# Gated slot attention with a Hadamard feed-forward on one core: VectorE's work around the quarter-array products in another order

## The chip, the cores and the metric

The kernel runs on one core of one Trainium2 chip. The metric is device time of one execution in microseconds (us). Before the change the median of three runs was 3658.88 us (3658.03 to 3659.67). TensorE is called PE, VectorE DVE, ScalarE ACT, GpSimd POOL and SyncE SP, as in the profile; SP issues all DMAs. "Lnnn" is line nnn of the kernel before the change.

## The reference, cut to what matters

The input x is 2 x 2048 x 512 in float32. The block is an attention, a layer norm over the sum with x, a feed-forward, and a second layer norm over that sum:

```python
q, k, s = heads of x@Wq, x@Wk, clip(x@Ws, -32, 32)     # 16 heads of 64
v, g    = heads of x@Wv, x@Wg                          # 16 heads of 128
# gated slot attention: two linear recurrences over time, a softmax between them
z  = cumlogsumexp(s); p = exp(s - z); decay = exp(z[t-1] - z[t])
hk = hk*decay + k p^T ;  ok = q hk ;  pv = softmax(ok)
hv = hv*decay + p v^T ;  o  = pv hv
o = rmsnorm(o)*g_norm_weight * silu(g)
x = layernorm(x + o@Wo)
h = fwht(silu(x@W1.T) * (x@W3.T))                      # Walsh-Hadamard, 2048 wide
out = layernorm(x + h@W2.T)
```

## The kernel before

**Products.** All large products are done by Strassen's scheme in Winograd's form, with 7 block products in place of 8 and two levels of it in the feed-forward. Each product therefore needs sums of blocks of its left and right factors. `Weights.sums(k)` makes the four sums of a weight (L416 to L422), `right_factor` those of an activation (L443 to L449: two copies on ACT, two differences on DVE, two on POOL).

**Stages.** Attention comes first, in 64 steps: 4 groups of 4 heads, 16 chunks of 128 tokens (of both batches) in each group. The output rows are kept in DRAM (`yd`) and added to group by group, so only the fourth group's steps finish a row: there `row_stats` (L86 to L91: two DVE instructions for each batch, then two short POOL instructions) and `normalize` (L95) do the layer norm, and `rows_transposed` (L914) or `rows_transposed_last` (L930) turn the rows for the feed-forward. Preparation of the feed-forward's weights (`up_weights` in group 0, `down_weights` after it) and of its input blocks (`block`, in group 3) is cut into pieces that are run inside the attention steps. The feed-forward (`up`, `down`) follows.

**Order.** The order on PE, DVE, ACT and POOL is exactly the order in which the code calls things; SP's is arranged by the framework. Each engine works through its queue in order. `run(new, now, before, old)` writes one iteration, in which four steps overlap: it loads for `new`, projects and scores `now`, finishes `before` (second recurrence, gate, transposition, first output products) and ends `old` (last output products, rows out). `main("q", k)` and `main("v", k)` are the seven products of the two projections (L519, L545), and everything else stands between them. `next(pieces[0])` runs one piece of preparation; an iteration has four such places, here called place 2 (after q2), 3 (after q5), 4 (after q6) and the end. In the last four chunks `more()` adds four places among the v products.

**The places that the change touches**, in the order of an iteration:

- q products, output products `old.o` 3, 6 and 7 (`o`, L754 is the DVE addition that empties their PSUM bank).
- `exp_s` (L527 on DVE, L531 and L533 on ACT, L532 on POOL), then v1, `load_rows`, `k_transposed` (L565), `old.o(4)`, `e_transposed` (L571) and `running_sum` (L578), which reads what L532 has written.
- "Quarter-array products": matmuls of 64 x 64 blocks (`scores` L596, `scores2` L669, `share_of_keys` L604, `slots` L622, `share_of_values` L679, `values` L690, `state_slots` L631, `state_values` L699), and the first half of `reciprocal` (L589).
- `gated`: ACT squares (L716), DVE multiplies by the gate (L718), `state` (L616 into `hv`), DVE sums the squares (L721), POOL makes the factor (L722, L723) and multiplies the gated values by it (L725).
- v6, v5, second `reciprocal`, v2, `row_stats` of `old`, v7, `softmax` (L639 reads the PSUM tile `pn`, L645, L647 on DVE, L648 on ACT), `store_rows` of `old` with `normalize`, v3, `softmax_sum` (L652, L653 on DVE, L654 on POOL).
- `o_transposed` (L742): PE transposes the gated values into PSUM and `right_factor` makes `ob` of them (L443 and L444 on ACT, L446 and L447 on DVE, L448 and L449 on POOL).
- `softmax_end` (L658), v4, `tanh`, `before.o` 1, 5, `silu` (L559), 2 (L758 is the matmul of all `o`).

**PSUM.** Two double banks `ps[0]` and `ps[1]` serve everything but the products' sums. `flat(0)` is all of `ps[0]`, `flat(2)` all of `ps[1]`. `pn`, which `softmax` reads, lies in `ps[1]`; so did the transposed gated values, `flat(2)`. `state` reads the second half of `ps[0]`. The products' sums rotate over four banks: `c1` (two), `c2` and `c3`; o1 uses c1, o5 and o3 c2, o2 c3.

Of the kernel before, what the change touches and what calls it, by code (L numbers as in the profile page):

```python
# [9 lines left out]
F32 = mybir.dt.float32  # L10
# [28 lines left out]
def gated_slot_attention_ffn_kernel(  # L39
# [43 lines left out]
    def row_stats(src):  # L83

        st = small.tile([P, 6], F32, name="st")
        nc.vector.bn_stats(st, src)  # L86
# [263 lines left out]
    with ExitStack() as att:  # L350
# [16 lines left out]
        def flat(at):  # L367
            return ps[at // 2].rearrange("p b (i t) -> p (b i) t", t=P)
# [22 lines left out]
        class Weights:  # L391
# [17 lines left out]

            def sums(self, k):  # L410
                t, low = self.t, self.low
                if k == 0:
                    if self.raw is not None:
                        self.raw(t[:, 0:3])
                        self.raw(low)
                    nc.vector.tensor_tensor(t[:, 3], low, t[:, 2], ALU.add)  # L416
                elif k == 1:
                    nc.vector.tensor_tensor(t[:, 5], t[:, 0], low, ALU.subtract)
                elif k == 2:
                    nc.vector.tensor_tensor(t[:, 4], t[:, 3], t[:, 0], ALU.subtract)  # L420
                else:
                    nc.vector.tensor_tensor(t[:, 6], t[:, 1], t[:, 4], ALU.subtract)  # L422

        def rows_of(src, g, width):
            return lambda j: src[j * HD : (j + 1) * HD, g * width : (g + 1) * width]
# [53 lines left out]
        class Step:  # L479
# [228 lines left out]
            def gated(self):  # L708

                sq = c1.tile([P, 2, NQ, DV], F32, name="sq", tag="big")  # L710
                self.gj = self.t2[:, :, HD:].rearrange("p q (j d) -> p j q d", d=DV)

                every = slice(0, P)
                moves = [(0, every, every), (1, HALVES[0], HALVES[1]), (1, HALVES[1], HALVES[0])]
                for j, to, at in moves:
                    nc.scalar.activation(sq[to, j], self.po[j][at], AF.Square)  # L716
                for j, to, at in moves:
                    nc.vector.tensor_tensor(self.gj[to, j], self.po[j][at], self.gj[to, j], ALU.mult)  # L718
                self.state()
                ss = small.tile([P, 2 * NQ], F32, name="ss")  # L720
                nc.vector.tensor_reduce(ss, sq.rearrange("p j q d -> p (j q) d"), AX.X, ALU.add)  # L721
                nc.gpsimd.tensor_scalar(ss, ss, 1.0 / DV, EPS, ALU.mult, ALU.add)  # L722
                nc.gpsimd.tensor_tensor(ss, ss, mhalf, ALU.pow)  # L723
                ssb = ss.rearrange("p (j q o) -> p j q o", j=2, o=1).to_broadcast([P, 2, NQ, DV])
                nc.gpsimd.tensor_tensor(self.gj, self.gj, ssb, ALU.mult)  # L725


            def load_rows(self):
                self.rows = []
                for b in range(2):  # L730
                    t = yp.tile([P, D], F32, name="rows", tag="rows")
                    n = self.n
                    nc.sync.dma_start(out=t, in_=yd[b * NCB + n] if self.g else x[b, n * P : (n + 1) * P, :])
                    self.rows.append(t)

            def o_transposed(self):
                tp = flat(2)
                for b in range(2):
                    for i in range(2):
                        for j in range(2):  # L740
                            at = HD + j * DV
                            nc.tensor.transpose(  # L742
                                tp[:, b * 4 + i * 2 + j, :], self.t2[:, 2 * i + b, at : at + DV], ident
                            )
                self.ob = c1.tile([P, 7, 2, P], F32, name="ob")
                right_factor(self.ob, tp)
# [13 lines left out]
                        start=(k in OPENS and c == 0), stop=(c == 1), skip_group_check=True,  # L760
                    )

            def row_stats(self):
                if self.g == NG - 1:
                    self.stats = [row_stats(t) for t in self.rows]

            def store_rows(self):
                for b in range(2):
                    if self.g == NG - 1:
                        normalize(self.rows[b], self.stats[b])  # L770
                    nc.sync.dma_start(out=yd[b * NCB + self.n], in_=self.rows[b])


# [23 lines left out]
        def up_weights():  # L797

            todo = [(p, i, half) for p in range(NSET) for i in range(2) for half in range(2)]

            def load(p, i, half):
                return [load_row((w1, w3)[i], p + NSET * (2 * half + q)) for q in range(2)]

            def inner(d, src, at, n):

                t = hp.tile([P, 4, 2, P], F32, name="inner", tag="h3", bufs=4)[:, :, 0:n]
                first_sums(nc.vector, t, *(src(r, c) for r in range(2) for c in range(2)))
                o = d[:, at : at + n].rearrange("p m k t -> p k m t")
                for c in range(2):
                    nc.sync.dma_start(out=o[:, c], in_=src(0, c))  # L810
                nc.sync.dma_start(out=o[:, 2], in_=src(1, 1))
                for k in range(4):
                    nc.sync.dma_start(out=o[:, 3 + k], in_=t[:, k])

            def inners(d, wt, outer):
                inner(d, lambda r, c: wt[:, 0, r, :, c], 0, 2)
# [5 lines left out]
                inner(d, lambda r, c: outer[:, 2:4, r, c], 5, 2)  # L822

            raws, rest = load(*todo[0]), iter(())

            both = hp.tile([P, 2, 2, 2, 2, 2, P], F32, name="both", tag="h1")
            for n, (p, i, half) in enumerate(todo):
                next(rest, None)
                yield
                wt = both[:, n // 2 % 2]  # L830
                tp = ps[1].rearrange("p q (c t) -> p q c t", t=P)
                for q in range(2):
                    for c in range(KC):
                        nc.tensor.transpose(tp[:, q, c], raws[q][:, c * P : (c + 1) * P], ident)
                nc.scalar.copy(wt[:, half].rearrange("p i a b t -> p i (a b) t"), tp)
                next(rest, None)
                yield
                next(rest, None)
                if half:
                    outer = hp.tile([P, 4, 2, 2, P], F32, name="outer", tag="h2")  # L840
                    first_sums(nc.vector, outer, *(wt[:, r, :, c] for r in range(2) for c in range(2)))
                    rest = inners(w13s[p][:, :, :, i], wt, outer)
                yield
                if n + 1 < len(todo):
                    raws = load(*todo[n + 1])
                yield
            for _ in rest:
                yield

        def down_weights():  # L850
# [3 lines left out]
            for pair in ((0, 2), (1, 3)):  # L854
# [39 lines left out]
                for hb in range(NPB):  # L894
# [9 lines left out]
                    nc.sync.dma_start(out=o[:, 3:7], in_=t)  # L904
                    if hb % 2:
                        yield

        def rows_transposed(step):

# [87 lines left out]
                yield  # L997
            yield from down_weights()

        y = {"second": False}  # L1000
        pieces = [work()]
        ups = None
        steps = [Step(g, n) for g in range(NG) for n in range(NCB)]
# [2 lines left out]
        def run(new, now, before, old):  # L1006
# [6 lines left out]
            def main(name, k):  # L1013
# [3 lines left out]
                elif before is not None:  # L1017
                    for _ in range(FILL[name, k]):
                        next(ups)

            def more():

                if old is not None and old.g == NG - 1 and old.n >= NCB - 4:
                    next(pieces[0], None)


            g = now.g if now is not None else NG
# [17 lines left out]
            next(pieces[0], None)  # L1045
            if changes:
                nw["vg"].sums(0)
            main("q", 5)
            next(pieces[0], None)
            if changes:  # L1050
                nw["vg"].sums(1)
            main("q", 6)
# [2 lines left out]
            if changes:  # L1055
                nw["vg"].sums(2)
            main("q", 7)
            next(pieces[0], None)
# [56 lines left out]
            more()  # L1115
            if o_opens:
# [138 lines left out]
```

## Time and profile before

| What | Value |
|---|---|
| median of three runs | 3658.88 us |
| the profiled execution's own time | 3661.32 us |
| its span | 3659.5 us |
| PE busy, share of the span | 3512.5 us, 96% |
| DVE busy | 2380.8 us, 65% |
| POOL, ACT busy | 1088.0 us (30%), 987.4 us (27%) |
| mean granted TensorE clock | 0.996 |
| attention / feed-forward | up to about 2580 us / the rest |

The busy shares say that PE is nearly always at work. What PE is not at work is 147 us, and the view of waits names the releaser of most of it. A group's "idle before" is the time that its engine stood still just before it, and the releaser is the instruction whose end let it go. All but a few of PE's waits lie in the attention steps, of which one lasts about 40 us.

### The profile page before, as it was taken

The page shows a single profiled execution, that of the slowest core. Times are in us where ns is not written, and L with a number is a line of the kernel's source. Part 1 is how long each engine was busy: PE and PEld are TensorE (multiplying, and loading weights), DVE is VectorE, ACT ScalarE, POOL GpSimd, SP SyncE. Part 2 cuts the span into 40 slices and gives each one's busy share as a digit, 9 for nine tenths or more (in the row PEclk, how much of TensorE's full clock was granted, in tenths as well). Part 3 has the DMA queues.
Part 4 walks back from the last instruction along what each step waited for, and adds up shares of the span by engine and source line. Part 5 has one row for each costly group of instructions (what it writes and reads, how often), then busy time and mean ns, then how long its engine had stood idle before and what let it go on. Part 6 is the DMA issues. An engine that isn't in the chain of part 4 may idle for free.

```text
span 3659.5 us, 76139 instructions
## 1 busy us (share of the span) xinstructions
PE 3512.5 (96%) x32160; PEld 2774.9 (76%) x32160; DVE 2380.8 (65%) x3976; ACT 987.4 (27%) x1768; POOL 1088.0 (30%) x1040
## 2 busy tenths in 40 slices
PE   8999999999999999999999999998899999999998
PEld 6777776677777767777766776776688888888887
DVE  5667667755667655667566567767666765765756
ACT  3333333333333333333333333332111111111110
POOL 2222222211212221213112222222344454453553
PEclk9999999999999999999999999999999999999999
DMA  4433443411121321122121232435646535435432
GB/s 152 124 111 103 129 128 110 130 62 59 60 68 54 118 70 58 60 68 82 53 88 57 68 108 87 152 132 190 230 135 222 196 119 211 158 120 211 157 123 82
DMA packets 229190, 425.10 MB, mean 116 GB/s; under 512 B 20592, under 2 KB 141808, under 8 KB 228848
## 3 DMA queue, kind: packets, MB, share of 16 engines
q1 hardware_dynamic: 228848, 420.22, 34.5%
q8 instruction: 253, 4.15, 0.5%
q14 instruction: 89, 0.73, 0.1%
HBM read 297.47 MB, written 125.30 MB: 116 GB/s over the span
## 4 chain that ended last, share of the span: by engine, by line
PE 75%; DVE 12%; POOL 5%; ACT 3%; issue 3%; DMA 1%; SPq 0%; POOLq 0%; DVEq 0%; ACTq 0%
PE c L235 17%; PE c L519 16%; PE dc L274 10%; PE c L758 10%; PE c L545 6%; ACT sq L716 3%; DVE t L718 2%; POOL t L725 2%; POOL ss L723 2%; DVE ss L721 2%; PE ps L679 2%; PE po L699 2%; PE po L690 2%; PE running L578 2%; PE ps L742 1%
## 5 line engine op out<-in xcount | busy, mean ns | idle before, releaser
L545 PE MATMUL c<-wvg,xb 128*128 128x512 f32 x1792 | 814.5, 600 | 2.4 <-DVE wvg L420 1.8
L545 PEld LDWEIGHTS c<-wvg,xb 128*128 128x128 f32 x1792 | 324.5, 191 | 365.5 <-issue 293.9
L519 PE MATMUL c<-xb,wqks 128*128 128x128 f32 x3584 | 550.3, 276 | 5.6 <-DVE t L477 2.4
L519 PEld LDWEIGHTS c<-xb,wqks 128*128 128x128 f32 x3584 | 481.5, 192 | 23.6 <-issue 8.1
L274 PE MATMUL dc<-w2t,hid 128*128 128x256 f32 x1792 | 455.3, 379 | 2.1 <-DVE res L281 2.1
L216 DVE TENSOR_TENSOR accux<-c,accux 128x512 f32<-128x512 f32 x496 | 340.9, 690 | 177.9 <-PE c L235 161.9
L235 PE MATMUL c<-wvg,xb 128*128 128x256 f32 x1792 | 432.0, 380 | 7.3 <-DVE accux L216 6.5
L754 DVE TENSOR_TENSOR rows<-c,rows 128x256 f32<-128x256 f32 x448 | 182.1, 417 | 351.0 <-PE c L758 350.9
L235 PEld LDWEIGHTS c<-wvg,xb 128*128 128x128 f32 x1792 | 338.7, 190 | 58.3 <-DVE accux L216 10.3
L274 PEld LDWEIGHTS dc<-w2t,hid 128*128 128x128 f32 x1792 | 340.2, 190 | 49.5 <-DVE res L281 3.3
L519 PE MATMUL c<-wqks,xb 128*128 128x128 f32 x1792 | 347.6, 276 | 1.1 <-DMA wqks<-in_L_attn_Ws 1.1
L477 DVE TENSOR_TENSOR t<-c,kept 128x384 f32<-128x384 f32 (+1 forms) x384 | 230.6, 609 | 165.1 <-PE c L519 157.8
L235 PE MATMUL c<-wqks,xb 128*128 128x256 f32 x1344 | 324.9, 380 | 6.8 <-DVE accv L216 2.5
L472 ACT COPY kept<-c 128x384 f32<-128x384 f32 (+1 forms) x384 | 203.1, 529 | 360.2 <-PE c L519 275.4
L532 POOL TENSOR_TENSOR e<-e,zc 1x512 f32<-1x512 f32 x60 | 75.9, 1264 | 754.4 <-ACT e L531 710.8
L235 PEld LDWEIGHTS c<-wqks,xb 128*128 128x128 f32 x1344 | 253.9, 190 | 45.7 <-DVE accux L216 5.2
L722 POOL TENSOR_SCALAR ss<-ss 128x8 f32<-128x8 f32 x64 | 13.1, 204 | 899.8 <-DVE ss L721 899.8
L519 PEld LDWEIGHTS c<-wqks,xb 128*128 128x128 f32 x1792 | 273.0, 193 | 1.4 <-DMA wqks<-in_L_attn_Ws 1.4
L281 DVE TENSOR_TENSOR res<-dc,res 128x256 f32<-128x256 f32 x448 | 188.8, 422 | 118.1 <-PE dc L274 107.3
L589 DVE RECIPROCAL iz<-z 128x256 f32<-128x256 f32 x128 | 223.2, 1744 | 0.0
L718 DVE TENSOR_TENSOR t<-po,t 64x512 f32<-64x512 f32 (+1 forms) x192 | 132.3, 689 | 122.1 <-ACT sq L716 121.3
L250 POOL TENSOR_TENSOR accw<-accw,accux 128x512 f32<-128x512 f32 x60 | 75.8, 1275 | 283.5 <-DVE accux L216 282.1
(194 smaller groups left out, 5116.7 us busy)
## 6 DMA issues: line engine op xcount, KB each, us to landing
xb<-w13s SPq DMA_DIRECT2D x112, 896.0 KB
xb<-xd SPq DMA_DIRECT2D x48, 896.0 KB
yd<-rows SPq DMA_DIRECT2D x128, 256.0 KB
w2t<-w2s SPq DMA_DIRECT2D x32, 896.0 KB
rows<-yd SPq DMA_DIRECT2D x100, 256.0 KB
xd<-xb SPq DMA_DIRECT2D x16, 896.0 KB
wvg<-fxd SPq DMA_DIRECT2D x16, 896.0 KB
raw<-in_L_ffn_W SPq DMA_DIRECT2D x48, 256.0 KB
```

What stands on the lines that cost most here:

```text
L216: nc.vector.tensor_tensor(into[:, b], s, (into if first is None else first)[:, b], ALU.add)
L235: nc.tensor.matmul(s[:, j * TQ : (j + 1) * TQ], lhsT=w[:, LEFT[k], j, :], rhs=right[:, RIGHT[k], :], start=(k in (1, 2, 5) and j == 0), st ...
L274: nc.tensor.matmul(s, lhsT=h["hid"][:, i, LEFT[m], k * P : (k + 1) * P], rhs=h["w2"][:, i, RIGHT[m], :], start=(m in (1, 2, 5) and i == 0) ...
L281: nc.vector.tensor_tensor(r, s, r, ALU.add)
L472: nc.scalar.copy(self.kept[k], s)
L477: nc.vector.tensor_tensor(t[:, to], s, self.kept[other], ALU.add)
L519: nc.tensor.matmul(out[:, i * P : (i + 1) * P], lhsT=a, rhs=b, start=(k in OPENS and c == 0 and i == 0), stop=(c == 1), skip_group_check=True,
L545: nc.tensor.matmul(out, lhsT=self.xb[:, RIGHT[k], c, :], rhs=w["vg"].t[:, LEFT[k], c, :], start=(k in OPENS and c == 0), stop=(c == 1), sk ...
L589: nc.vector.reciprocal(self.iz[:, h], self.z[:, h])
L718: nc.vector.tensor_tensor(self.gj[to, j], self.po[j][at], self.gj[to, j], ALU.mult)
L754: nc.vector.tensor_tensor(y_, self.uo.sum(k), y_, ALU.add)
L758: nc.tensor.matmul(out, lhsT=self.ob[:, RIGHT[k], c, :], rhs=w["o"].t[:, LEFT[k], c, :], start=(k in OPENS and c == 0), stop=(c == 1), ski ...
```

## The change

Six things are different.

1. `gated`: the sum of squares (L721) goes ahead of `state` (L616).
2. `o_transposed`: the gated values are transposed into `flat(0)`, not `flat(2)`.
3. `row_stats` is called for one batch at a time: for batch 1 right after `old.o(7)`, ahead of `exp_s`, for batch 0 right after `old.o(4)`. `normalize` becomes a call of its own, and it and `store_rows` go from behind `softmax` to behind the first half of `reciprocal`. As before, statistics and normalization happen in group 3 alone; the store, in all groups.
4. `Weights.sums`: for Wo, and only for it, sums 1 and 3 are made on POOL.
5. `up_weights`: of a pair of halves, the first sums, which stood together at place 4 (four instructions), are split over the end of the iteration and place 2 of the next; the inner sums follow at place 3, the end, place 2 and place 3. Place 4 has none. The whole preparation ends one iteration later.
6. `down_weights`: the pieces of the last sums skip place 4.

```diff
@@ Weights.sums
+                second = nc.vector if self.raw is None else nc.gpsimd
...
-                    nc.vector.tensor_tensor(t[:, 5], t[:, 0], low, ALU.subtract)
+                    second.tensor_tensor(t[:, 5], t[:, 0], low, ALU.subtract)
...
-                    nc.vector.tensor_tensor(t[:, 6], t[:, 1], t[:, 4], ALU.subtract)
+                    second.tensor_tensor(t[:, 6], t[:, 1], t[:, 4], ALU.subtract)
@@ gated
-                self.state()
                 ss = small.tile([P, 2 * NQ], F32, name="ss")
                 nc.vector.tensor_reduce(ss, sq.rearrange("p j q d -> p (j q) d"), AX.X, ALU.add)
+                self.state()
@@ o_transposed
-                tp = flat(2)
+                tp = flat(0)
@@ row_stats, store_rows
-            def row_stats(self):
+            def row_stats(self, b):
                 if self.g == NG - 1:
-                    self.stats = [row_stats(t) for t in self.rows]
+                    self.stats[b] = row_stats(self.rows[b])
+
+            def normalize(self):
+                if self.g == NG - 1:
+                    for b in range(2):
+                        normalize(self.rows[b], self.stats[b])

             def store_rows(self):
                 for b in range(2):
-                    if self.g == NG - 1:
-                        normalize(self.rows[b], self.stats[b])
                     nc.sync.dma_start(out=yd[b * NCB + self.n], in_=self.rows[b])
@@ up_weights
-            def inners(d, wt, outer):
+            def sums(d, wt):
+
+                outer = hp.tile([P, 4, 2, 2, P], F32, name="outer", tag="h2")
+                a11, a12, a21, a22 = (wt[:, r, :, c] for r in range(2) for c in range(2))
+                nc.vector.tensor_tensor(outer[:, 0], a21, a22, ALU.add)
+                nc.vector.tensor_tensor(outer[:, 2], a11, a21, ALU.subtract)
+                yield
+                nc.vector.tensor_tensor(outer[:, 1], outer[:, 0], a11, ALU.subtract)
+                nc.vector.tensor_tensor(outer[:, 3], a12, outer[:, 1], ALU.subtract)
+                yield
+                inner(d, lambda r, c: wt[:, 1, r, 1:2, c], 2, 1)
+                yield
+                inner(d, lambda r, c: outer[:, 0:2, r, c], 3, 2)
+                yield
+                inner(d, lambda r, c: outer[:, 2:4, r, c], 5, 2)
+                yield
                 inner(d, lambda r, c: wt[:, 0, r, :, c], 0, 2)
...
                 next(rest, None)
                 yield
+
+                yield
+                if half:
+                    for _ in rest:
+                        pass
+                    rest = sums(w13s[p][:, :, :, i], wt)
                 next(rest, None)
-                if half:
-                    outer = hp.tile([P, 4, 2, 2, P], F32, name="outer", tag="h2")
-                    first_sums(nc.vector, outer, *(wt[:, r, :, c] for r in range(2) for c in range(2)))
-                    rest = inners(w13s[p][:, :, :, i], wt, outer)
-                yield
@@ down_weights
                     if hb % 2:
                         yield
+                        if y["place"] == 3:
+                            yield
@@ run
             do(old, "o", 7)
+            do(old, "row_stats", 1)
...
             do(old, "o", 4)
+            do(old, "row_stats", 0)
...
             do(now, "reciprocal", 0)
+            do(old, "normalize")
+            do(old, "store_rows")
             do(before, "values")
...
-            do(old, "row_stats")
...
             do(now, "softmax")
-            do(old, "store_rows")
```

More of the change, by code (lines that the diff above doesn't have):

```diff
@@ L728, in load_rows @@
             def load_rows(self):
-                self.rows = []
+                self.rows, self.stats = [], {}
                 for b in range(2):
@@ L813, in inner @@
                     nc.sync.dma_start(out=o[:, 3 + k], in_=t[:, k])
-            def inners(d, wt, outer):
-                inner(d, lambda r, c: wt[:, 0, r, :, c], 0, 2)
+            def sums(d, wt):
[6 more added lines that the diff above has]
+                nc.vector.tensor_tensor(outer[:, 3], a12, outer[:, 1], ALU.subtract)
                 yield
@@ L822, in inners @@
                 inner(d, lambda r, c: outer[:, 2:4, r, c], 5, 2)
+                yield
+                inner(d, lambda r, c: wt[:, 0, r, :, c], 0, 2)
             raws, rest = load(*todo[0]), iter(())
@@ L846, in up_weights @@
                 yield
-            for _ in rest:
+            for place in range(4):
+                if place != 2:
+                    next(rest, None)
+                yield
+            for place in range(4):
+                if place != 2:
+                    next(rest, None)
                 yield
@@ L998, in work @@
             yield from down_weights()
-        y = {"second": False}
+        y = {"second": False, "place": 0}
         pieces = [work()]
@@ L1019, in main, with work_on @@
                         next(ups)
+            def work_on(place):
+                y["place"] = place
+                next(pieces[0], None)
             def more():
                 if old is not None and old.g == NG - 1 and old.n >= NCB - 4:
-                    next(pieces[0], None)
+                    work_on(1)
             g = now.g if now is not None else NG
@@ L1044, in run @@
             y["second"] = new is not None and new.g > 0
-            next(pieces[0], None)
+            work_on(2)
             if changes:
@@ L1048, in run @@
             main("q", 5)
-            next(pieces[0], None)
+            work_on(3)
             if changes:
@@ L1057, in run @@
             main("q", 7)
-            next(pieces[0], None)
+            work_on(4)
             if changes:
```

## The prediction

> **What bounds the kernel now.** I read the page's busy shares first: PE works 96% of the span, so a change on other engines can only give back what PE stands still, and the view of PE's waits prices that. Columns: waiting line, releaser, total us, times, longest.
>
> ```profile
> PE ps L742 <- DVE r L639: 35.2, 17, 5.1
> PE ps L742 <- POOL t L725: 17.1, 42, 0.4
> PE c L758 <- DVE ob L446: 11.1, 15, 2.7
> PE ps L631 <- issue: 11.1, 10, 2.6
> ```
>
> Two of the three upper lines are waits of the transposition L742 that the change attacks: for softmax's reading of `ps[1]` and for the gated values. The timeline splits them into kinds. An ordinary step of groups 0 to 2:
>
> ```profile
> 1032.81 1.90 POOL L725 TENSOR_TENSOR t<-t,ss 128x1024 f32<-128x1024 f32 x1
> 1033.44 0.68 DVE L639 TENSOR_TENSOR r<-ps,iz 128x512 f32<-128x512 f32 x1
> ...
> 1034.76 1.09 PE L742 MATMUL ps<-ident,t 128*128 128x128 f32 x8 [0.38 <-POOL t L725]
> ```
>
> and one of group 3, with the statistics in DVE's queue ahead of softmax:
>
> ```profile
> 2202.81 0.68 DVE L86 BATCH_NORM_STATS2 st<-rows 128x6 f32<-128x512 f32 x1
> ...
> 2205.01 0.68 DVE L639 TENSOR_TENSOR r<-ps,iz 128x512 f32<-128x512 f32 x1
> ...
> 2205.83 1.06 PE L742 MATMUL ps<-ident,t 128*128 128x128 f32 x8 [1.50 <-DVE r L639]
> 2206.73 1.88 PE L545 MATMUL c<-wvg,xb 128*128 128x512 f32 x4
> 2207.05 1.00 DVE L95 TENSOR_SCALAR rows<-rows,mv,lrs 128x512 f32<-128x512 f32 x2
> 2207.22 0.63 ACT L648 ACTIVATE r<-r 128x512 f32<-128x512 f32 x1 [7.43 <-DVE r L647]
> 2207.76 0.57 ACT L443 COPY ob<-ps 128x512 f32<-128x512 f32 x1
> ```
>
> The last two lines matter most: the copy L443 that makes o1's factor stands behind softmax's exponential L648 in ACT's queue, and L648 waits for DVE's L647. So even if L742 waits for softmax no longer, o1, four matmuls later, still waits for DVE through ACT. A freed L742 is worth only what that chain leaves.
>
> **The change part by part.** All times are of the profiled execution (3661.3 us; 2.4 above the median 3658.9; the differences are carried over).
>
> *A. Squares ahead of `state`, ordinary steps.* `state` (L616, 0.69) no longer stands ahead of L721, so the factor and L725 end about 0.6 us sooner; `state` comes 1.1 later and only empties half of `ps[0]`, next written by L742 itself 3 us on. In the step shown, the values are there at 1034.1 and PE is free at 1034.38: the 0.38 goes. What is late next: v4 then ends at 1037.03; `ob` L443 ends at 1036.77 as before, and o1 starts 0.12 after such an end (2208.33 to 2208.45). L446 ends at 1037.55, o5 needs it at 1037.9. Both fit, by 0.1 and 0.3. So 41 waits go whole: 17.1 less the 0.34 of the last, **-16.8**. Bounds: if the DVE chain slips by 0.15 only 0.24 a step is left (-10); nothing here can gain more.
>
> *B. Statistics and normalization moved, group 3.* Twelve steps wait 1.50 to 1.87 for L639 (sum 18.6) and 0.32 each for L446 at o5 (3.8). With the two pairs of L86 and L88 gone from the queue (2202.81 to 2204.42, 1.61 us) L647 ends at 2205.5 and L443 at 2206.7, o1 could start at 2206.83 and PE is there at 2206.95; without L95 (0.91) ahead of it L446 ends at 2207.5, o5 needs it at 2207.8. So 22.4 go. They are paid in another place. Batch 1's pair (0.82, and 0.1 for waiting on the end of L754) now stands ahead of `exp_s` L527, and what waits behind it is L531, L532 and `running_sum` L578, and L533 and `e_transposed`:
>
> ```profile
> 2186.19 0.63 ACT L531 ACTIVATE e<-e 128x512 f32<-128x512 f32 x1 [1.24 <-DVE e L527]
> 2186.90 1.27 POOL L532 TENSOR_TENSOR e<-e,zc 1x512 f32<-1x512 f32 x1 [14.23 <-ACT e L531]
> ...
> 2188.59 1.03 PE L578 MATMUL running<-e,causal 128*128 128x256 f32 x4
> ```
>
> L532 ends at 2188.17 and L578 starts at 2188.59: 0.37 of slack with 0.05 for the signal. L527 comes 0.94 later, so L578 waits 0.57; L571 takes 0.33 of that earlier. On POOL the pair L90, L91 (0.19 and 0.54) now stands ahead of L532, but ends at 2187.6, before the late L531 (2187.8): nothing. Batch 0's pair falls between o4 (L754 at 2188.36) and L598 (1.63 idle before it); both L95 fall into the 0.95 that DVE waits for L716: covered, the second by almost nothing. The stores go to SP some 10 us sooner with their rows. 12 x 0.57 = 6.8, so 18.6 + 3.8 - 6.8 = **-15.6**. Bounds of the price: 0 to 1.5 a step (all of 0.94, and POOL's pair last): -22 to -4.
>
> *C. Steps 16 of groups 0 to 2* (three waits of 2.51 for L639, behind the sums of the next Wq). The wait only moves:
>
> ```profile
> 640.14 0.63 ACT L648 ACTIVATE r<-r 128x512 f32<-128x512 f32 x1 [8.43 <-DVE r L647]
> 640.68 0.57 ACT L443 COPY ob<-ps 128x512 f32<-128x512 f32 x1
> 641.37 2.78 PE L758 MATMUL c<-wo__234,ob 128*128 128x256 f32 x12
> ```
>
> L647 is as late as before and o1 starts at 641.37 either way: **0**, PE standing before o1 for some 2.5 us in place of L742.
>
> *D. Wo's sums on POOL, three group openings.* DVE loses L418, which took 1.74 while POOL ran L654 (its like, L416, took 0.69 alone), so L446 comes 1.65 sooner and o5's waits of 1.77, 2.74 and 2.74 shrink. But POOL then has, after L654 (ends 1968.40), sum 1 (1.27, from the 128x512 row of L654), L448 (0.73), L449 (1.06) and sum 3 (1.27): 1972.8, and o3 reads sum 3. Before, o3 started at 1973.09. Three openings: **-1**; bounds -7 (POOL not late) to +3. On this, the Trainium skill, SBUF - State Buffer, section "Who interferes with whom", says that a DVE instruction with two SBUF inputs contends with a GpSimd instruction that reads SBUF: a rule against this move, which agrees with the 1.74. Taken as an exclusive lock it would put another 1.27 on DVE at each opening, +3 in place of -1 (an estimate).
>
> *E. The last two chunks with waits of 5.09 and 4.01*, in which `block` adds to DVE. After the first, PE ran at half speed for two stretches of 3.4 us (the page's windows give a clock of 0.61 for 2488.5 to 2495.5, L742 1.94 in place of 1.06), and so after the second: 8.5 and 7.4 lost in all. With the statistics gone and L742 free, o1 waits for L443, 3.5 and 2.5 us by the same chain, then 0.2 and 0.35 at o5; in the first, `e_transposed` waits already (0.36), so that 0.85 is paid there. With one half-speed stretch (1.7) or two after the 3.5 and one in two chances of one after the 2.5: 7.0 and 4.3, **-4.5**; bounds 0 and -10. The Trainium skill, TensorE: Matmul & The Clock Gate, section "What's actually happening", has the gate close only after a whole idle window of 3413 ns. By it the second chunk would lose nothing more and E would be -5.4 (an estimate). This trace has half-speed stretches after waits of 1.97, 2.17 and 2.52, and none after two of 2.51: I go by the trace.
>
> *F. `up_weights` and `down_weights`.* The four sums at place 4 delayed no PE wait in group 0. Moved to the end, two (1.28) or four (1.65) instructions stand ahead of o3's L754, which frees `c2` for q5. In an ordinary step L754 of o2 ends at 485.33 and q5 starts at 487.95; with 1.65 and 0.4 for o3's L754, `c2` is free at 487.45: covered by 0.5. At the change to group 1 the new Wq's sums fill that place and there is no transposition of x: o3's L754 is late by 0.7 there, and place 3's inner sums go ahead of a wait that costs 1.02 now (1.6 more). **+2.5**; bounds 0 and +12 (0.7 in each of 16 steps). `down_weights` has no wait of PE to its name: 0.
>
> Sum: -16.8 - 15.6 + 0 - 1 - 4.5 + 2.5 = -35.4. PE's waits for "issue" (38 us) may fall elsewhere, by some 4 us either way. 3661.3 - 35.4 = 3625.9 for a profiled execution, 3658.9 - 35.4 = **3623.5** for the median.
>
> **The rivals.**
> - *The DVE chain takes back more* (0.22). A leaves 0.24 a step (-10), the price at `exp_s` is 0.94 (22.4 - 11.3 = -11), E gives nothing, F +2.5: -18, 3641. For it: o1's margin of 0.1 after L443; against it: L647's place in the queue does not change in groups 0 to 2.
> - *More goes than I count* (0.12). B is paid for by less (the 0.33 of L571 alone: -18), D gives its -7, and the half-speed stretches after the long waits go (E -10), F 0: -52, 3607. For it: those stretches followed PE's waits; against it: POOL's row of five instructions before o3.
> - *Slower: the pieces at the iteration's end* (0.08). In group 0, `c2` for q5. The same inner sums took 0.84 and 0.95 in place of 0.42 beside POOL's work (489.71); four of these are 3.4 against 1.65, past the margin of 0.5 by 1.2, and with a half-speed stretch (1.7) by 2.9 a step. It decides from 38 / 16 = 2.4 us in each of 16 steps: 3658.9 - 38 + 46 = 3667. Against it: POOL is idle from 483.79 on in that place.
> - *No difference* (0.04): A's chain held by something that the view of waits put down to L725 only because it came last, and B paid back whole: within 7 us of 3659.
>
> **How the numbers follow.** The forecast (-28 to -43) has 0.54. What a measurement of this kernel can tell from no change is 0.2%, 7.3 us; the forecast, the first two rivals and nearly nothing else lie beyond it: faster 0.87, same 0.05, slower 0.08. The range reaches from the larger gain (3607) to a little past the first rival (3646), and leaves out the slower case and the no-difference one.
>
> **What would show each step.** A: waits of L742 for L725 near 0 in place of 42. B: L742's waits for L639 gone, new waits of L571 and L578 of 0.3 to 0.6 in twelve steps. C: PE's weight load L758 waiting some 2.5 us for L443. D: o3 waiting for POOL's sum in three places. E: waits of 3.5 and 2.5 before o1, with a clock under 1. F: no waits of q5 in group 0. I am wrong if L758's waits for L443 or L446 come up in ordinary steps, if L578 waits over 1 us, or if q5 waits for L754.

## The result, and the profile after

The changed kernel takes 3631.65 us (median of four runs, 3630.56 to 3633.43) against 3658.45 (3654.34 to 3659.67) for the kernel before on the same chip, four runs as well: ratio 0.9929, 95% interval 0.9912 to 0.9946, or 27 us less. The forecast was 3623.5, 8 us lower; its range reached from 3607 to 3646. The band that had the chance of 0.54, 28 to 43 us less, ends 1 us short of what was measured. The profiled execution of after took 3630.56 us (span 3628.6) against 3661.32 (span 3659.5): 30.8 us less, which is what the sums below are held against.

Up to the edits, lines of after stand two lower than those of before: L742 is now L744, L758 is L760, L443 is L445, L754 is L756, L639 is L641, L725 is L727. In a later place, L859 has become L880.

The view of PE's waits of after (waiting line, releaser, total us, times, longest):

```profile
PE c L760 <- ACT ob L445: 5.8, 5, 1.3
PE c L760 <- DVE rows L756: 5.5, 4, 1.7
PE c L521 <- DVE rows L756: 5.0, 7, 1.9
PE c L760 <- POOL wo__6781 L424: 3.5, 1, 3.5
PE c L760 <- POOL wo__17921 L424: 3.3, 1, 3.3
PE c L760 <- POOL wo__12382 L424: 2.5, 1, 2.5
...
PE ps L744 <- POOL t L727: 0.3, 1, 0.3
PE ps L573 <- ACT e L535: 0.9, 3, 0.3
```

The two lines that carried the forecast, 35.2 us of L742 for softmax and 17.1 for the gated values, are gone: one wait of 0.3 is left. In their place stand three waits for POOL's fourth sum of Wo (9.3 together), and q2 (L521) and o1 (L760) wait for DVE and ACT. With o5's waits for L446 (11.1 before, 0.4 now) the view lists some 63 us less of these kinds and some 19 more of those just named (in all 100 us in place of 139), and the time fell by 31.

A step of group 3 in after, in the timeline, answers to the group 3 lines of the prediction:

```profile
2187.43 1.07 PE L744 MATMUL ps<-ident,t 128*128 128x128 f32 x8
...
2206.69 0.69 DVE L86 BATCH_NORM_STATS2 st<-rows 128x6 f32<-128x512 f32 x1
2207.52 0.39 DVE L529 TENSOR_SCALAR e<-t 128x512 f32<-128x512 f32 x1
2208.01 0.63 ACT L533 ACTIVATE e<-e 128x512 f32<-128x512 f32 x1 [2.16 <-POOL lrs L90]
2208.71 1.26 POOL L534 TENSOR_TENSOR e<-e,zc 1x512 f32<-1x512 f32 x1
2209.35 0.42 PEld L573 LDWEIGHTS ps<-ident,e 128*128 128x128 f32 x4 [0.54 <-ACT e L535]
2210.03 0.73 PEld L580 LDWEIGHTS running<-e,causal 128*128 128x128 f32 x4 [0.26 <-POOL e L534]
```

L744 starts without a wait. The statistics L86 now stand ahead of L529, and the price is there too: the weight loads of `e_transposed` (L573) and of `running_sum` (L580) wait for ACT and POOL.

An ordinary step of group 1 in after:

```profile
1025.98 1.05 PE L744 MATMUL ps<-ident,t 128*128 128x128 f32 x8
1027.97 0.57 ACT L445 COPY ob<-ps 128x512 f32<-128x512 f32 x1
1028.59 2.46 PEld L760 LDWEIGHTS c<-wo__6781,ob 128*128 128x128 f32 x12 [0.67 <-ACT ob L445]
...
1032.02 1.21 DVE L561 SCALAR_TENSOR_TENSOR t<-th,t 128x1024 f32<-128x1024 f32 x1
1033.15 0.96 DVE L756 TENSOR_TENSOR rows<-c,rows 128x256 f32<-128x256 f32 x2
1033.62 0.52 PEld L521 LDWEIGHTS c<-xb,wqks 128*128 128x128 f32 x4 [0.37 <-DVE rows L756]
```

The 0.38 before the transposition is gone. But q2, some 7.6 us later, now waits for DVE: L756 empties the PSUM bank that q2 writes, and stands behind `silu` (L561, 1.21 us) in DVE's queue. PE got there sooner, DVE did not. The view of weight loads (PEld) counts how often. Before:

```profile
PEld c L519 <- DVE rows L754: 5.1, 10, 0.7
```

and after:

```profile
PEld c L521 <- DVE rows L756: 20.1, 42, 2.1
PEld c L760 <- ACT ob L445: 46.8, 61, 2.1
PEld ps L573 <- ACT e L535: 8.4, 15, 0.8
PEld running L580 <- POOL e L534: 4.0, 15, 0.3
```

42 weight loads of the q products wait where 10 did, 39 of them q2's. In the 40 ordinary steps of groups 0 to 2 it is 33 in place of 2; the other eight before stood at the changes of groups and in the last chunks. PE's own waits show 7: at most of these stalls the matmul beside them is listed as busy (o3's, 1032.62 to 1033.65 in the step above).

**Where the 31 us went, stage by stage.** Cutting each step at the first weight loads of k's transposition, the transposition of the gated values, o1, q1 and r's transposition, and adding over steps (us, profiled executions):

| steps | before | after | difference | forecast |
|---|---|---|---|---|
| ordinary, groups 0, 1 and 2 (14 + 13 + 13) | 558.9 + 498.9 + 493.2 | 554.6 + 494.1 + 491.0 | -11.4 | A and F: -14.3 |
| group 3, twelve steps | 477.9 | 460.0 | -17.9 | B: -15.6 |
| three group openings | 132.3 | 133.2 | +0.9 | D: -1 |
| the two steps ahead of each opening | 244.7 | 246.1 | +1.4 | C: 0 |
| last two chunks, to the product o3 of the second | 91.8 | 86.8 | -5.0 | E: -4.5 |

Together -32.0; the remaining 1 us lies in the beginning and the feed-forward. Two executions of one kernel differ by up to 3.6 us in a cell of this table (a second one of after gave 551.2 + 490.8 + 490.8 and 136.8).

Nearly all of that difference in the ordinary steps lies in one stage, the quarter-array products from `scores` to the first v product behind them, where the view lists PE's waits for "issue": 258.1 us before, 255.1 and 247.7 in the two profiles of after, for 40 steps. Everything else in these steps repeats: 1293.0 us before (1293.2 and 1293.4 in the runs below of the bank alone and of the statistics alone), 1284.6 and 1285.1 in the two profiles of after. Sums "without that stage" below are made this way.

### The profile page after: what moved, and what is told of

Its sections match the earlier page's. It is cut to its first block, busy times and chain, and to the rows that moved or that the text cites. A ratio compares the mean times of both kernels' runs of the same rounds, so it can differ in the third digit from the quotient of the medians.

```text
span 3628.6 us, 76147 instructions
## 1 busy us (share of the span) xinstructions
PE 3517.6 (97%) x32160; PEld 2770.5 (76%) x32160; DVE 2380.9 (66%) x3968; ACT 983.7 (27%) x1768; POOL 1108.4 (31%) x1048
## 5 line engine op out<-in xcount | busy, mean ns | idle before, releaser
L521 PE MATMUL c<-xb,wqks 128*128 128x128 f32 x3584 | 555.9, 278 | 6.2 <-DVE rows L756 5.0
L521 PEld LDWEIGHTS c<-xb,wqks 128*128 128x128 f32 x3584 | 481.4, 193 | 34.4 <-DVE rows L756 20.1
L756 DVE TENSOR_TENSOR rows<-c,rows 128x256 f32<-128x256 f32 x448 | 182.5, 418 | 345.7 <-PE c L760 344.1
L521 PE MATMUL c<-wqks,xb 128*128 128x128 f32 x1792 | 348.7, 277 | 1.5 <-DMA wqks<-in_L_attn_Ws 1.5
L521 PEld LDWEIGHTS c<-wqks,xb 128*128 128x128 f32 x1792 | 273.9, 193 | 1.8 <-DMA wqks<-in_L_attn_Ws 1.8
L720 DVE TENSOR_TENSOR t<-po,t 64x512 f32<-64x512 f32 (+1 forms) x192 | 132.3, 689 | 107.3 <-ACT sq L718 106.4
```

Source lines behind the costliest of these rows:

```text
L521: nc.tensor.matmul(out[:, i * P : (i + 1) * P], lhsT=a, rhs=b, start=(k in OPENS and c == 0 and i == 0), stop=(c == 1), skip_group_check=True,
L756: nc.vector.tensor_tensor(y_, self.uo.sum(k), y_, ALU.add)
```

## The experiments

In all of them the time is compared with the kernel before, run on the same chip; a 95% interval stands in brackets. The changed kernel itself was run once more beside the first three: 3627.61 us, ratio 0.9925 [0.9913, 0.9937].

### Wo's sums back on VectorE

```diff
-                second = nc.vector if self.raw is None else nc.gpsimd
+                second = nc.vector
```

> The changed kernel with Wo's sums 1 and 3 back on VectorE. My theory, that o3 now waits for GpSimd's sum 3 at the three group openings (3.5, 2.5, 3.3 us, and one half-speed stretch of 3.4 us lost): those waits go, VectorE's wait before o5 of 1.8 to 2.7 us comes back, about 4 us faster than the changed kernel (1 to 7), so 31 us under before. Rival, that the move paid, as the wait of o5 says: 5 to 7 us slower than the changed kernel. No difference if both waits weigh the same.

Measured: 3616.65 us, 0.9898 [0.9885, 0.9911], 11 us under after on the same chip. The move to POOL does not gain, it costs, by the medians more than was expected (4, at most 7). Lines of an opening of after, in the timeline:

```profile
719.81 1.27 POOL L656 TENSOR_TENSOR r<-r,iz 128x512 f32<-128x512 f32 x1 [1.41 <-DVE sm L654]
720.51 1.12 DVE L422 TENSOR_TENSOR wo__6781<-wo__6781 128x512 f32<-128x512 f32 x1
721.05 1.71 POOL L420 TENSOR_TENSOR wo__6781<-wo__6781,low 128x512 f32<-128x512 f32 x1
721.56 1.75 DVE L660 TENSOR_TENSOR r<-r,sm 128x512 f32<-128x512 f32 x1
722.72 1.18 POOL L450 TENSOR_TENSOR ob<-ob 128x256 f32<-128x256 f32 x1
723.98 1.72 POOL L451 TENSOR_TENSOR ob<-ob 128x256 f32<-128x256 f32 x1
725.65 1.44 POOL L424 TENSOR_TENSOR wo__6781<-wo__6781 128x512 f32<-128x512 f32 x1
727.14 1.13 PE L760 MATMUL c<-wo__6781,ob 128*128 128x256 f32 x4 [3.49 <-POOL wo__6781 L424]
```

and the same opening with the sums on DVE:

```profile
714.77 1.27 POOL L656 TENSOR_TENSOR r<-r,iz 128x512 f32<-128x512 f32 x1 [1.41 <-DVE sm L654]
714.84 1.75 DVE L420 TENSOR_TENSOR wo__6781<-wo__6781,low 128x512 f32<-128x512 f32 x1
716.98 3.62 PE L760 MATMUL c<-wo__6781,ob 128*128 128x256 f32 x8 [1.78 <-DVE ob L448]
717.00 0.72 POOL L450 TENSOR_TENSOR ob<-ob 128x256 f32<-128x256 f32 x1 [0.96 <-DVE ob L448]
717.80 1.05 POOL L451 TENSOR_TENSOR ob<-ob 128x256 f32<-128x256 f32 x1
718.31 1.09 DVE L424 TENSOR_TENSOR wo__6781<-wo__6781 128x512 f32<-128x512 f32 x1
721.77 1.03 PE L760 MATMUL c<-wo__6781,ob 128*128 128x256 f32 x4
```

In the first, sums 1 and 3 and `ob`'s two differences stand one behind another on POOL and take 6.05 us; the same kinds of instruction had been priced at 1.27 + 0.73 + 1.06 + 1.27 = 4.33. With the sums on DVE, L450 and L451 are back at 0.72 and 1.05. o5 waits 1.78 instead, and o3 for no sum. The three openings take 126.8 us against 133.2 and 136.8 in the two profiles of after; without the stage of the quarter-array products 106.0 against 110.2 and 115.0, or 4 to 9 of the 11 us.

### The statistics of batch 1 behind `exp_s`

```diff
             do(old, "o", 7)
-            do(old, "row_stats", 1)
...
             do(now, "exp_s")
+            do(old, "row_stats", 1)
```

> The changed kernel with batch 1's statistics behind the clamp of s instead of ahead of it. My theory, that group 3's fourteen steps pay 0.65 us each from the first transposition to the scores because the clamp, the exponentials and the running sum start 0.94 us late: 7 to 9 us faster than the changed kernel. Rival, that this is hidden (the waits listed for the matmuls there are 0.3 us, three times in all): within 1.5 us of it.

Measured: 3617.29 us, 0.9896 [0.9883, 0.9909], 10 us under after. The stage from k's transposition to the scores falls from 45.46 us in twelve steps (second profile of after) to 37.49, what it was before the change. So the price of the statistics ahead of `exp_s` was 0.66 a step, and it is the place in the queue that costs, not the statistics: behind `exp_s` they cost nothing in this stage.

### Output product 2 ahead of `silu`

```diff
-            do(now, "silu")
             do(before, "o", 2)
+            do(now, "silu")
```

> The changed kernel with VectorE's addition of o2 ahead of its silu (1.21 us). My theory, that in the ordinary steps of groups 0 to 2 the freed time was taken back where q2's first weight load waits 0.37 us for bank c3, which the addition of o2 empties behind silu: those 40 waits go, 0.2 to 0.3 us a step, 8 to 11 us faster than the changed kernel. Rival, that those waits lie beside matmuls still running and that the moved pieces of weight preparation cost what is missing: within 2 us of the changed kernel.

Measured: 3622.59 us, 0.9909 [0.9896, 0.9922], 5 us under after, about half of what was expected. The two intervals overlap, so the time alone does not show a gain; the stages do. The weight loads of the q products that wait for L756 fall from 42 (20.1 us) to 15 (9.7 us). The stage of q2 takes 0.22 us less a step in group 0 and 0.15 less in group 1, and hardly less in group 2 (0.06). One of the last two chunks took 2.0 more.

### The transposition's bank alone, and with the squares

The first has one edit to the kernel before, the second adds the other:

```diff
             def o_transposed(self):
-                tp = flat(2)
+                tp = flat(0)
```

```diff
-                self.state()
                 ss = small.tile([P, 2 * NQ], F32, name="ss")
                 nc.vector.tensor_reduce(ss, sq.rearrange("p j q d -> p (j q) d"), AX.X, ALU.add)
+                self.state()
```

> The kernel before with the gated values transposed into the other double bank, and nothing else. Read from the view of waits alone: the 35.2 us for which the transposition waits for softmax go, 30 to 38 us faster than before. My theory: o1 starts as late as before, since its factor's copy stands behind softmax's exponential on ScalarE; the waits move from the transposition to o1's weight load (about 1.4 us in group 3's steps, 2.5 in the last step of a group), and the time is within 4 us of before.

> The kernel before with the other bank and with the sum of squares ahead of state. My theory: against the run with the bank alone, the 42 waits of 0.41 us for GpSimd's gated values go, of which 0.1 a step stays before o1 and some of the rest is taken back at q2: 8 to 14 us faster than before, nearly all of it in groups 0 to 2, and group 3 no better than 1 us. Read from the waits alone: 50 us faster.

Measured: the bank alone 3663.59 us, 1.002 [1.001, 1.0031]; both 3644.22 us, 0.9968 [0.9958, 0.9979]. With both edits the time is as expected (12 us less by the ratio); with the bank alone it is 0.2% above the kernel before, 4 to 11 us, where within 4 was expected. One step of group 3 with the bank alone (lines of before):

```profile
2240.90 1.09 PE L742 MATMUL ps<-ident,t 128*128 128x128 f32 x8 [0.42 <-POOL t L725]
2244.82 3.16 PE L758 MATMUL c<-wo__17921,ob 128*128 128x256 f32 x12 [1.12 <-ACT ob L443]
```

and with both edits:

```profile
2227.47 3.17 PE L758 MATMUL c<-wo__17921,ob 128*128 128x256 f32 x12 [1.53 <-ACT ob L443]
```

Here, whatever the time, the wait of L742 for softmax (1.50 to 1.87 a step before) is seen to move: 0.42 and 1.12 with the bank alone, 1.53 at o1 with both. L443 stands behind L648 in ACT's queue, and L648 behind DVE's softmax, whichever bank L742 writes. An undisturbed step of group 3 (mean of the first eight) takes 40.0 us in all three kernels. Whoever reads the 35.2 us of waits for L639 as the worth of another bank is wrong by all of it here.

### The squares alone

The second edit above without the first.

> The kernel before with one edit: the squares and their sum ahead of state, the transposition still in ps[2]. Mine: the bank does nothing, so this alone is as good as both together: waits of L742 for L725 near 0 in groups 0 to 2, group 3 unchanged (L742 waits 1.5 to 1.9 for L639), -8 to -13 us. Rival 1 (the bank alone costs 8 us by its median, and squares and bank together gain 11, so the squares are worth 19): -16 to -22. Rival 2 (the squares need the other bank): within 4 us of before.

Measured: 3642.78 us, 0.9951 [0.9938, 0.9963], -18 on this chip, with an interval of -14 to -23: in the range of the first rival (-16 to -22), and more than was expected (-8 to -13). The view of PE's waits:

```profile
PE ps L742 <- DVE r L639: 31.0, 17, 4.1
```

L742's waits for L725 are gone from that view, as with the bank, and those for softmax in group 3 are not. By the mean step of the profiles, both kernels give the same in groups 0, 1 and 2: 39.7, 37.9 and 37.7 us with the squares alone, 39.6, 37.9 and 37.7 with both, 39.9, 38.4 and 37.9 before. Without the stage of the quarter-array products the 40 ordinary steps take 1281.4 us in both, 11.6 less than before. So what the squares gain in these steps does not need the other bank. What speaks for the rival's reason, that the bank alone costs some 8 us, are times: the two ratios differ by 0.17%, and the bank alone came out 0.2% above the kernel before. The profile of the bank alone has one stage longer by 2.2 us, where a DMA of `block` came late, and the first of the last two chunks longer by 1.1, and nothing that recurs from step to step; whether the bank costs a few us without the other edits stays open.

### Statistics and normalization alone

The kernel before with `row_stats(0)`, `row_stats(1)`, `normalize` and `store_rows` in the places they have in after.

> The kernel before with one edit: statistics and normalization in their new places, the transposition still in ps[2] and behind the old order of the gate. Mine (DVE's queue held L742 in group 3, the bank did not): without the two pairs of BATCH_NORM ahead of it L639 ends some 1.6 us sooner, near 2204.1 where PE is ready at 2204.3, so each of the twelve steps keeps only the 0.4 for L725 that an ordinary step has; 18.6 + 3.8 - 12 x 0.41 - 12 x 0.66 = -9.5, and some -3 in the last two chunks: -8 to -14 us. Rival (the bank is needed too, since ps[2] must be read by softmax first): L742 goes on waiting over 1 us for L639 in group 3, and with the price at exp_s the time falls by less than 4 us or rises.

Measured: 3643.44 us, 0.9956 [0.9942, 0.997], -16 (-11 to -21), a little more than the -8 to -14 expected.

```profile
PE ps L742 <- POOL t L725: 22.4, 54, 0.4
PE ps L742 <- DVE r L639: 11.8, 5, 3.5
```

Twelve waits of some 0.4 for L725 have taken the place of those for L639, as expected; the five left for L639 are steps 16 and the last two chunks. The twelve steps of group 3 fall from 477.9 to 466.6 us, with the price at `exp_s` paid. The bank was not what held L742 there, DVE's queue was. The other 6.6 us that group 3 gains in after come with the squares: from the first v product behind the quarter-array products to L742 a step of group 3 takes 9.27 us here and 8.69 in after, 7.0 us in twelve.

### The bank put back

After with `flat(2)` in place of `flat(0)`, nothing else.

> The kernel after with the transposition back in ps[2] and nothing else. Mine: softmax's reading ends ahead of PE in every ordinary step once statistics and squares have moved, so the time stays within 5 us of after; L742 waits about 2.5 for L639 at steps 16 of groups 0 to 2 and 2.5 to 3.5 in the last two chunks, where o1 then waits for L445 no longer. Rival (the other bank is what took softmax off the path): waits of over 0.5 for L641 in group 3, 8 to 20 us slower than after.

Measured: 3630.89 us, 0.9922 [0.9909, 0.9936]; after had 0.9925 [0.9913, 0.9937].

```profile
PE ps L744 <- DVE r L641: 8.7, 6, 2.5
```

Six waits of L744 for softmax come back, and o1's waits for L445 leave the view of PE's waits in their place. The twelve steps of group 3 take 461.0 us against 460.0. With the rest of the change in place, the other bank does nothing that can be measured (each interval is some 5 us either way).

### The pieces alone

The kernel before with `up_weights` and `down_weights` in their new places.

> The kernel before with the pieces of weight preparation in their new places alone (up_weights, down_weights). My theory: these cover themselves but for 2 us at the change to group 1: between 0 and 4 us slower than before. Rival, that they are what took back the missing part of the forecast: 6 to 12 us slower.

Measured: 3656.07 us, 1.0 [0.9991, 1.0009]: no difference beyond 3 us either way.

```profile
PE c L519 <- DVE rows L754: 3.7, 8, 1.1
```

q5 waits for L754 in no ordinary step, but by 1.06 and 0.19 at the change to group 1 and by 0.80 at the change to group 2, where it did not before. In group 2 the moved pieces lengthen the stage from r's transposition to k's by 0.4 us a step (88.7 to 93.9 in thirteen) and shorten the one before it by 0.3 (95.3 to 91.8): work moved from one place to the next, not quite for nothing. Without the stage of the quarter-array products, the ordinary steps take 1294.5 us against 1293.0.

### The three repairs together

After with Wo's sums on DVE, product 2 ahead of `silu`, and the statistics of batch 1 behind `exp_s`.

> The changed kernel with three steps undone or turned at once: Wo's sums on VectorE, o2's addition ahead of silu, batch 1's statistics behind the clamp. If the gains of the three runs before (11, 5 and 10 us) lie in different places, as their parts of a step say, they add up to about 24 us against the changed kernel: some 50 us under before, ratio 0.985 to 0.988. If they hide each other, no better than the best of the three, ratio 0.990.

Measured: 3605.72 us (3602.37 to 3606.27), 0.9864 [0.9851, 0.9878]: 50 us under the kernel before. By the ratios this is 0.61% under after, 22 us, where the three single gains add up to 26. It beats both kernels.

```profile
PE c L521 <- DVE rows L756: 6.8, 8, 2.2
...
PE c L760 <- DVE ob L448: 5.3, 3, 1.8
```

The three waits for POOL's sums are gone and o5's three of 1.78 are back (L448). Group 3's twelve steps are at 452.3 us.

## Why the prediction was right in sign and 8 us too low

The runs of single edits account for the change: squares -18, statistics -16, pieces 0, Wo's sums on POOL +10 and the bank nothing that shows beside the rest make -24, for -27 measured (each run is known to some 3 to 6 us).

**A, squares ahead of `state`: the mechanism right, too large.** The 41 waits went whole, as said. PE reaches the transposition some 0.57 us sooner by its matmuls (0.60 by its weight loads) in each ordinary step, more than the 0.41 that the view showed. But a step gains only 0.30, 0.37 and 0.17 us in the three groups: 0.10 is taken back at o1 where o1 follows L445 (2.69 against 2.59 in group 0), and 0.25 at q2. The step that failed is the sentence "What is late next": it followed ACT to o1 and DVE to o5 and found both in time (o1 by 0.1, which a gain of 0.57 used up), and stopped there. The next instruction that PE needed of DVE was L756 behind `silu`, a q product later, with some 0.14 us of slack in an ordinary step: in group 0 PE is at o3 0.49 sooner, and from o3 to q2's weight load it takes 0.35 longer. The experiment with product 2 ahead of `silu` takes back 0.22 of those 0.25 in group 0. Without the stage of the quarter-array products the squares are worth -11.6 (the two runs with them give 0.25, 0.35 and 0.27 a step), near the lower bound, 0.24 a step and -10, but for another reason than the one it was given for. That the squares alone came out at -18 by time is more than these steps show; what the rest is was not followed.

**B, statistics and normalization: right, and a little too small.** 18.6 of waits at L742 and 3.8 at o5 gone; the price at `exp_s` 0.66 a step (8.0 in twelve) for a forecast of 0.57 (6.8). The gain is -17.9 against -15.6, since the stages of L742 and o5 shrank by more than the waits shown (at o5 by 0.56 a step where the view gave 0.32). The prediction did not ask which of its edits did this; the runs of single edits show that the queue did and the bank did not, and that 6.6 of it comes with the squares.

**C, steps 16 of groups 0 to 2: right.** The wait moved: 2.51 at L742 became 1.25 before o1, with the weight load waiting 2.1 for L445. From the first v product behind the quarter-array products to o1 these three steps take 13.32 us each where they took 13.98, 15.68 and 13.98; in the second a half-speed stretch had followed the wait (1265.2 us, 3.4 long). So 3.7 us are gained that the zero left out. The row of the table is up by 1.4 because the stage of the quarter-array products is longer in three of the six steps; without that stage the row falls by 2.9, and by 1.4 in the second profile of after.

**D, Wo's sums on POOL: the side was seen, the size not.** The forecast was -1, with o3 waiting for POOL's sum in three places. It does, by 3.49, 2.50 and 3.32 us, and the openings gave +0.9 and, in another profile of the same kernel, +4.5. The failed term is POOL's row of instructions at 4.33: each of them began here while an instruction of DVE was under way, and the row took 6.05 (the last section has the reason). On DVE the same openings gave -5.4 (-1.6 without the stage of the quarter-array products). The rule of the Trainium skill that was weighed there (SBUF - State Buffer, section "Who interferes with whom"), taken as an exclusive lock, had given +3 as an estimate, nearer to what was measured than the -1 that the forecast used; the rows agree with such a lock, but it was POOL's row that paid, where the estimate had put the price on DVE.

**E, the last two chunks: right in sum, wrong in place.** -5.0 against -4.5. The waits of 3.5 and 2.5 before o1 are only 1.26 and 0.74; q5 and a product of the feed-forward wait 1.86 and 1.80 for L756 instead. Of four half-speed stretches one is left, behind another wait. These waits (9.1 before, 5.7 now) and three stretches of 1.7 would make -8.5; what took 3.5 of it back among `block`'s work was not followed.

**F, the pieces: about the size forecast, in another place.** The time of the pieces alone, 0 within 3 us, does not tell 0 from +2.5. At the change of groups q5 does wait for L756 in after, 1.06 and 0.80, but the wait of 1.02 that stood later in these steps is gone: the stage from r's transposition to k's falls from 8.33 and 8.16 to 7.19 and 7.06. In the ordinary steps, without the stage of the quarter-array products, the pieces alone cost 1.5, and after takes 3.2 to 3.7 more than the squares alone, some 0.12 in each step of groups 1 and 2, where the forecast had put 0. Which edit does this beside the squares was not tried; the pieces are what is left to suspect.

**The rivals.** The first (the DVE chain takes back more) named A's lower figure rightly, but its other parts did not come. The slower one (q5 waits for `c2` in group 0) is refuted by the run of the pieces alone, where no ordinary step has that wait. Two of the signs named for being wrong did come up, without the forecast falling by them: o1's weight load waits for L445 in ordinary steps by 0.67 us in place of 0.24 (it costs the 0.10 above), and q5 waits for L756 at two changes of groups. By the table, A and F are 3 us short of the forecast, C and D 3 more, and B and E give back 3; the profiles differ by 30.8 and the medians by 26.8, since the profiled execution of before was 2.9 us above its median and that of after 1.1 below.

## What to carry to other kernels

When a wait is taken off the busiest engine, follow that engine for the whole loop, not to the next two waits: every place where another engine has less slack than the wait is worth takes back a part. The views of waits before the change do not show these places: q2's weight load waited in 2 of the 40 ordinary steps before and in 33 after. The slack has to be read from the timeline. A PSUM bank named in a wait need not be the bound: look at which in-order queue the releaser stands in, since another bank leaves that queue as it is. Work moved to an idle engine is priced by that engine's durations beside the one it is meant to relieve, not by its durations alone. Before a stage's sum is read from two profiles, find the stages that differ between two profiles of one kernel, and leave them out.

## What the hardware showed that was not expected

- **A wait of 3.5 us before the same product brought half speed in one execution and not in another.** The timeline of the first profile of after, behind the wait of the opening shown above:

```profile
728.11 0.61 PE L521 MATMUL c<-xb,wqks 128*128 128x128 f32 x4
728.55 0.39 PE L521 MATMUL c<-wqks,xb 128*128 128x128 f32 x2
```

and of the second profile of the same kernel:

```profile
722.05 2.08 PE L760 MATMUL c<-wo__6781,ob 128*128 128x256 f32 x4 [3.50 <-POOL wo__6781 L424]
723.92 1.06 PE L521 MATMUL c<-xb,wqks 128*128 128x128 f32 x4
724.77 0.63 PE L521 MATMUL c<-wqks,xb 128*128 128x128 f32 x2
```

The same matmuls take 0.61 and 0.39 in the one and 1.06 and 0.63 in the other, and the granted clock is 1.00 from 728 to 732 in the one and 0.50 from 724 to 728 in the other. The wait of 2.5 at the second opening likewise was followed by full speed in the first and by 0.80 and 0.77 in the second. The Trainium skill, TensorE: Matmul & The Clock Gate, section "What's actually happening", has the gate close after a whole idle window of 3413 ns. The waits of 2.5 and 3.5 agree with it only in part: the length of a wait alone decides neither way. It moves the openings' sum by some us between two executions, and leaves a term like D or E uncertain by 1.7 or 3.4 for each long wait.
- **Stalls are partly hidden in busy time.** A stage of o5 gained 0.56 us where the view of PE's waits showed 0.32, and the transposition was reached some 0.57 sooner where it showed 0.41. The weight-load waits of the same places were longer than PE's own.
- **DVE and POOL take turns at sums of two operands: the one that began second ends a fixed time after the other has ended.** DVE's sum of 128 x 512 float32 for a weight takes 0.69 us alone. In all 100 cases in the runs of this case where a two-operand instruction of POOL was under way when it began, it ended 0.54 to 0.55 us after POOL's, whether that made it 1.75 us long (714.84 to 716.59 above, POOL's L656 from 714.77 to 716.04) or 0.75. POOL's L656, which had begun first, took its usual 1.27. The other way round, POOL's sum L420 ended 1.13 after DVE's L422 (721.63 to 722.76) and took 1.71 in place of 1.27. So in these rows neither advances while the other is at work, the one that began first is not lengthened, and the order in which they begin decides which engine pays.
